# A graph-network kernel on one core: two VectorE steps of its quantile stage cut into pieces of one slot

## The chip, the cores and the metric

The kernel runs on one core of one Trainium2 chip. The metric is the device time of one execution in microseconds (us). Engine names in the profile: PE is TensorE, DVE is VectorE, ACT is ScalarE, POOL is GpSimd, SP is SyncE, which here issues plain DMAs.

## What is computed

Sixteen graphs of 1024 nodes with 64 features each go through four layers. Each layer normalises `x`, clips it at zero and adds the layer's result to `x`. The first three layers are products with the dense 1024 x 1024 matrix `adj` and small weights. The fourth is the one that the change touches:

```python
adj_d = _dilate_adj(adj, mask)      # drops some neighbours of nodes that have more than 10
agg = _weighted_nanquantile_agg(x, adj_d > 0)
out = (1.0 + EPS_GIN) * x + agg
h = jax.nn.relu(jnp.einsum('bnc,ch->bnh', out, W1) + b1)
y = jnp.einsum('bnh,ho->bno', h, W2) + b2
return y * mask[..., None].astype(dtp)
```

The aggregate is, for each node and each feature, the sum 0.25 q(0.25) + 0.5 q(0.5) + 0.25 q(0.75) of interpolated quantiles over the node's remaining neighbours. Neighbours that were dropped count as very large values and sort to the end.

## The kernel before, in words

**Stages.** Six generators yield operations one by one: `listing` makes each node's list of neighbours from rows of `adj` (DVE: `max`, `match_replace`); `transposing` turns blocks of `adj` (PE, ACT); two `layering` workers run layers 1 to 3 for even and odd graphs (mostly PE and ACT) and store a table of features and a payload per graph; `gathering` fetches neighbours' rows from that table with indirect DMAs issued from POOL (80 per graph, one for each of 10 slots and 8 node tiles); `quantiling` sorts and weighs what was gathered; `dense`, added for each graph, multiplies and adds the weighed slots on PE, applies the two small matrices and stores the output.

**The order.** A planner, class `Weave`, holds a cost for every operation (DVE: 0.125 us + elements/960 in most cases; a gather 1.33 us) and lays out each engine's order ahead of time: it issues on the engine that can start first, and among operations that can start within 0.1 us it takes the one with the lowest key. So a change of an operation's length can move other operations on any engine. Where it plans a gap on PE it fills 90% of it with matmuls on a spare bank (line 567). A gather is given a wait on the latest PE instruction that other engines depend on and that the plan has ended before the gather's start (called the leash below). All waits for data come on top.

**Buffers.** Two `G` buffers take turns for the gathered slots, four `pay` buffers hold a graph from the load of `x` to its output, so that the load for graph b + 4 follows the output of graph b; two `row` buffers take rows of `adj` for the listing.

**The quantile stage.** `quantiles` works on cells of 128 nodes x T tiles x 64 features per slot. For a whole graph T is 8 and there are 11 slots, so one slot is 512 elements per partition. First comes `hits`, which finds the dropped neighbours; then their slots get 1e30 added ("bad,G" in the profile); a sorting network of `min` and `max` follows between `G` and `net`; `coef` is computed, and the slots that can hold a quantile are multiplied by it ("G,coef"). The last three places of a whole graph are weighed on ACT (`SHARE`), the others on DVE; `c["weighed"]` tells `dense` how far this has come. After the 16 graphs the nodes whose list stays longer than 11 go through the same stage once more, in four groups (`MANY`): T = 1, 2, 4, 2 with 23, 15, 13, 13 slots. Their outputs are scattered by POOL (line 1245).

**Lengths.** `LONGEST` = 1024 elements bounds a DVE instruction of this stage: `few` = 1024/(T x 64) slots, which is two for T = 8. `parts(k)` cuts k slots into pieces of at most `few`, and it is used for the addition and for the network's steps; the weighing uses `few` by itself.

Of the kernel before, what the change touches and what calls it, by code (L numbers as in the profile page):

```python
# [24 lines left out]
NT = N // P  # L25
# [79 lines left out]
SHARE = 3  # L105
# [349 lines left out]
class Fast:  # L455
# [623 lines left out]
    def quantiles(self, c):  # L1079

        V, S = self.V, self.S
        T, n, PS, G = c["T"], c["n"], c["PS"], c["cells"]

        def small(name, *shape):
            size = int(np.prod(shape))
            t = self.small(name, (P, self.sizes[name]))[:, 0:size]
            return t if len(shape) == 1 else t.rearrange("p (a b) -> p a b", b=shape[1])


        hits = small("hits", (n - 1) * T, 2)  # L1090
        yield V.tensor_tensor(hits.rearrange("p (k t) i -> p k t i", t=T), G[:, 1:n, :, C:R],
                              PS[:, None, :, SELF:SELF + 1].to_broadcast([P, n - 1, T, 2]), op=ALU.is_equal)
        flat = small("bad", (n - 1) * T)
        bad = flat.rearrange("p (k t) -> p k t", t=T)
        yield V.tensor_add(flat, hits[:, :, 0], hits[:, :, 1])
        m1 = small("m1", T)
        yield V.tensor_reduce(m1, bad.rearrange("p k t -> p t k"), axis=AX.X, op=ALU.add)
        yield V.tensor_sub(m1, PS[:, :, COUNT], m1)
        yield S.activation(G[:, 0, :, :], PS[:, :, H:H + R], AF.Copy)


        few = max(1, int(LONGEST / (T * C)))

        def parts(k):
            count = -(-k // few)
            return [slice(k * i // count, k * (i + 1) // count) for i in range(count)]

        for part in parts(n - 1):
            some = slice(part.start * T, part.stop * T)
            there = G[:, 1 + part.start:1 + part.stop, :, 0:C].rearrange("p k t c -> p (k t) c")  # L1110
            yield V.scalar_tensor_tensor(there, flat[:, some, None].to_broadcast([P, some.stop - some.start, C]), BIG, there,
                                         op0=ALU.mult, op1=ALU.add)
        net = yield "net"
        bufs = [w[:, 0:k * T * R].rearrange("p (k f) -> p k f", k=k) for w, k in ((c["G"], n), (net, EXTRA // T))]

        cells = [v.rearrange("p k (t c) -> p k t c", c=R) for v in bufs]


        places = max(int(np.ceil(tau * (n - 1))) for tau in TAUS) + 1
        pos = small("pos", T, 4)  # L1120
        yield V.tensor_tensor(pos, self.taus[:, None, :].to_broadcast([P, T, 4]),
                              m1[:, :, None].to_broadcast([P, T, 4]), op=ALU.mult)
        off = small("off", places, T * 4)
        yield V.tensor_tensor(off, getattr(self, f"place{n}", self.place)[:, 0:places, None].to_broadcast([P, places, T * 4]),
                              pos.rearrange("p t i -> p (t i)")[:, None, :].to_broadcast([P, places, T * 4]),
                              op=ALU.subtract)
        yield S.activation(off, off, AF.Abs)
        yield S.activation(off, off, AF.Relu, bias=1.0, scale=-1.0)

        def side(which, at, ap):  # L1130
            st, d1, n1, d2, n2 = ap
            st += at
            v = bufs[which]
            if n2 == 1:
                return v[:, st, :]
            inner = lambda s: v[:, s:s + d2 * (n2 - 1) + 1:d2, :]
            if n1 == 1:
                return inner(st)
            whole = v[:, st:st + d1 * n1, :] if st + d1 * n1 <= n else None
            if whole is None:  # L1140
                return None
            return whole.rearrange("p (a b) c -> p a b c", b=d1)[:, :, 0:d2 * (n2 - 1) + 1:d2, :]

        if n in NETWORKS:
            for op, k, *sides in NETWORKS[n]:
                for part in parts(k):
                    a, b, o = (cells[st // n][:, st % n + part.start * step:st % n + (part.stop - 1) * step + 1:step, :, 0:C]
                               for st, step in sides)
                    yield V.tensor_tensor(o, a, b, op=getattr(ALU, op))
            self.weave.give("net", net)  # L1150
            where = [(0, SORTED[n][0] + k) for k in range(places)]
        else:
            ops, at = network(n, places)
            for op, ap, dist, ba, bb, bo in ops:
                f = getattr(ALU, op)
                o = (bo, 0 if op == "min" else dist)
                aps = [side(ba, 0, ap), side(bb, dist, ap), side(*o, ap)]
                if any(v is None for v in aps):
                    st, d1, n1, d2, n2 = ap
                    for i in range(n1):  # L1160
                        one = (st + i * d1, 0, 1, d2, n2)
                        yield V.tensor_tensor(side(*o, one), side(ba, 0, one), side(bb, dist, one), op=f)
                else:
                    yield V.tensor_tensor(aps[2], aps[0], aps[1], op=f)
            where = [(at[k], k) for k in range(places)]

        coef = small("coef", places * T)
        yield V.tensor_reduce(coef, off.rearrange("p k (t i) -> p (k t) i", i=4), axis=AX.X, op=ALU.add)
        self.weave.add(self.dense(c, bufs, net, where), c["key"] - 1.0)
        k = 0  # L1170
        while k < places:
            e = k
            while e < places and where[e][0] == where[k][0]:
                e += 1
            e = min(e, k + few)
            v = bufs[where[k][0]][:, where[k][1]:where[k][1] + e - k, :].rearrange("p k (t c) -> p (k t) c", c=R)[:, :, 0:C]
            if T == NT and k >= places - SHARE:
                for i in range((e - k) * T):
                    yield S.activation(v[:, i, :], v[:, i, :], AF.Copy, scale=coef[:, k * T + i:k * T + i + 1])
            else:  # L1180
                yield V.tensor_mul(v, v, coef[:, k * T:e * T, None].to_broadcast([P, (e - k) * T, C]))
            k = e
            c["weighed"] = k
# [718 lines left out]
```

## Time and profile before

| what | value |
|---|---|
| median of 3 runs | 2494.44 us |
| lowest and highest | 2476.52, 2508.35 us |
| profiled execution, its own time | 2479.22 us |
| span in that profile | 2477.4 us |
| mean granted TensorE clock | 0.882 |
| gathers of G from the table on POOL | 1402, from 152 us to 2411 us |
| first and last load of x | 6 and 1795 us |
| table of graph 15 stored | 2039 us |
| gathers of graph 15 | 2080 to 2200 us |
| last `hits` and last `coef` on DVE | 2413.7 and 2457.6 us |

The profile comes from one execution. A row of a group gives line, engine, operation, output and inputs by the program's names, shape and count; then busy time in us and the mean duration of one in ns; then idle time just ahead of it on its engine and what ended most of it. All operations that the planner issues show its line 288, so groups are told apart by tile names. A row of waits gives who waited for whom, the total in us, the number of times and the longest. A row of the timeline gives start, length (of several merged instructions together), engine and operation.

### The profile page before, as it was taken

The page shows a single profiled execution, that of the slowest core. Times are in us where ns is not written, and L with a number is a line of the kernel's source. Part 1 is how long each engine was busy: PE and PEld are TensorE (multiplying, and loading weights), DVE is VectorE, ACT ScalarE, POOL GpSimd, SP SyncE. Part 2 cuts the span into 40 slices and gives each one's busy share as a digit, 9 for nine tenths or more (in the row PEclk, how much of TensorE's full clock was granted, in tenths as well). Part 3 has the DMA queues.
Part 4 walks back from the last instruction along what each step waited for, and adds up shares of the span by engine and source line. Part 5 has one row for each costly group of instructions (what it writes and reads, how often), then busy time and mean ns, then how long its engine had stood idle before and what let it go on. Part 6 is the DMA issues. An engine that isn't in the chain of part 4 may idle for free.

```text
span 2477.4 us, 28435 instructions
## 1 busy us (share of the span) xinstructions
PE 2168.9 (88%) x8704; PEld 955.1 (39%) x8704; DVE 1796.3 (73%) x4505; ACT 935.2 (38%) x2714; POOL 1595.6 (64%) x1441
## 2 busy tenths in 40 slices
PE   8999899999898979897988898989898887779857
PEld 3344334343443333434342434342433333334414
DVE  5878687878696878787878877887777484447553
ACT  4444444354444353535353535353534211101000
POOL 1037676767675767676766676776676677777670
PEclk9999898889897989898989898999897887889969
DMA  6345526262626262616252525262522112121110
GB/s 211 111 112 155 115 65 136 57 138 64 121 74 137 56 160 49 149 39 155 56 133 53 139 65 134 60 146 49 140 38 36 23 35 27 23 28 29 23 24 5
DMA packets 265406, 208.68 MB, mean 84 GB/s; under 512 B 78208, under 2 KB 225984, under 8 KB 265248
## 3 DMA queue, kind: packets, MB, share of 16 engines
q1 hardware_dynamic: 218368, 157.32, 23.3%
q0 software_dynamic: 46096, 48.62, 13.0%
q8 instruction: 72, 1.18, 0.2%
q10 hardware_dynamic: 784, 0.86, 0.1%
q14 instruction: 86, 0.70, 0.1%
HBM read 187.51 MB, written 19.17 MB: 83 GB/s over the span
## 4 chain that ended last, share of the span: by engine, by line
PE 61%; DVE 14%; issue 7%; another core or an unknown queue 7%; ACT 7%; DMA 3%; POOL 1%; SPq 0%; ACTq 0%; DVEq 0%; POOLq 0%
PE bank L288 49%; PE bank L567 13%; DVE G L288 5%; DVE net L288 3%; ACT sq L288 2%; DVE cand L288 1%; DMA block<-in_adj 1%; ACT wide L288 1%; DVE hn L288 1%; DMA pay<-in_x 1%; ACT nodes L288 1%; ACT G L288 1%; DVE st L288 1%; DVE pay L288 1%
## 5 line engine op out<-in xcount | busy, mean ns | idle before, releaser
L613 POOL DMA_INDIRECT G<-table,pay x1402 | 1564.9, 1116 | 812.9 <-issue 374.3
L567 PE MATMUL bank<-ones 128*128 128x512 f16 x2705 | 676.4, 399 | 57.4 <-issue 55.7
L288 PE MATMUL bank<-AT,nodes 128*64 128x512 f32 x2048 | 645.9, 650 | 38.8 <-ACT nodes L288 21.2
L567 PEld LDWEIGHTS <-ones 128*128 128x128 f16 x2705 | 267.6, 102 | 412.6 <-issue 162.8
L288 PEld LDWEIGHTS bank<-AT,nodes 128*64 128x64 f32 x2048 | 171.5, 146 | 374.8 <-issue 286.3
L288 ACT ACTIVATE sq<-pay,st 128x64 f32<-128x64 f32 x512 | 177.1, 346 | 130.1 <-DVE st L288 65.5
L288 DVE MAX8 cand<-key 128x8 f16<-128x128 f16 x1024 | 214.4, 279 | 5.7 <-DVE key L288 2.1
L288 ACT ACTIVATE AT<-bank 128x512 f32<-128x512 f32 x256 | 148.3, 591 | 177.5 <-PE bank L288 131.1
L288 ACT ACTIVATE wide<-bank 64x512 f32<-64x512 f32 x128 | 75.6, 591 | 359.8 <-PE bank L288 253.6
L288 PE MATMUL bank<-c,block 128*128 128x128 f32 x976 | 185.7, 313 | 21.1 <-ACT AT L288 9.1
L288 DVE TENSOR_TENSOR G<-G 128x1024 f32<-128x1024 f32 (+7 forms) x215 | 187.2, 903 | 2.6
L288 PEld LDWEIGHTS bank<-c,block 128*128 128x128 f32 x976 | 127.5, 158 | 159.4 <-issue 135.5
L288 DVE SCALAR_TENSOR_TENSOR key<-row,c 128x1024 f16<-128x1024 f32 x124 | 150.2, 1211 | 38.0 <-DMA row<-in_adj 29.3
L288 PE MATMUL bank<-G,c 128*128 128x512 f32 (+3 forms) x382 | 165.0, 571 | 14.0 <-DVE G L288 7.1
L288 ACT ACTIVATE nodes<-pay,off,ri 128x64 f32<-128x64 f32 x384 | 148.8, 430 | 36.1 <-DVE off L288 15.8
L288 DVE TENSOR_TENSOR yo<-bank,pay 128x256 f32<-128x256 f32 (+2 forms) x36 | 14.8, 411 | 181.5 <-PE bank L288 97.6
L288 DVE TENSOR_TENSOR net<-G 128x1024 f32<-128x1024 f32 (+7 forms) x140 | 141.1, 1033 | 1.3
L288 ACT ACTIVATE G<-G,coef 128x64 f32<-128x64 f32 x384 | 93.8, 336 | 96.8 <-DVE coef L288 96.7
L288 DVE TENSOR_TENSOR G<-net 128x512 f32<-128x512 f32 (+12 forms) x123 | 110.2, 939 | 1.2
L288 DVE MAX8 L<-cand 128x8 f16<-128x64 f16 x384 | 87.4, 228 | 29.2 <-remote 9.7
L288 PE MATMUL bank<-wide,wg 64*64 64x512 f32 (+1 forms) x192 | 105.1, 628 | 3.6 <-ACT wide L288 3.4
L288 DVE TENSOR_TENSOR G<-G,net 128x1024 f32<-128x1024 f32 (+5 forms) x113 | 104.4, 960 | 1.4
(176 smaller groups left out, 2238.4 us busy)
## 6 DMA issues: line engine op xcount, KB each, us to landing
row<-in_adj SPq DMA_DIRECT2D x124, 512.0 KB
block<-in_adj SPq DMA_DIRECT2D x122, 512.0 KB
G<-table,pay POOLq DMA_INDIRECT x1402
rows<-pay SPq DMA_DIRECT2D x16, 632.0 KB
G<-in_adj SPq DMA_DIRECT2D x10, 512.0 KB
table<-pay SPq DMA_DIRECT2D x16, 264.0 KB
pay<-in_x SPq DMA_DIRECT2D x16, 256.0 KB
out<-yo SPq DMA_DIRECT2D x16, 256.0 KB
```

What stands on the lines that cost most here:

```text
L288: return Op(self, lambda: f(*args, **kwargs), writes, reads, cost, later)
L567: weave.spare = (self.T, lambda: nc.tensor.matmul(busy, ones[:, 0:P], ones[:, 0:512], start=True, stop=True), [busy], [ones], 0.22)
L613: return self.nc.gpsimd.indirect_dma_start(out=out, out_offset=None, in_=table, in_offset=bass.IndirectOffsetOnAxis(ap=at, axis=0))
```

## The change

A second bound `alone` is half of `few`. The addition for dropped neighbours is cut by `alone`, and so is DVE's part of the weighing; the sorting network keeps `few`, and so does ACT's part of the weighing, which is done tile by tile anyway. For a whole graph the addition's pieces go from two slots (1024 elements) to one (512), and DVE's six weighed places from three instructions to six. For the four groups of long lists `alone` is 8, 4, 2 and 4 slots, where `few` was 16, 8, 4 and 8.

```diff
         few = max(1, int(LONGEST / (T * C)))
-
-        def parts(k):
+        alone = max(1, few // 2)
+
+        def parts(k, few):
             count = -(-k // few)
             return [slice(k * i // count, k * (i + 1) // count) for i in range(count)]
 
-        for part in parts(n - 1):
+        for part in parts(n - 1, alone):
             some = slice(part.start * T, part.stop * T)
...
             for op, k, *sides in NETWORKS[n]:
-                for part in parts(k):
+                for part in parts(k, few):
...
-            e = min(e, k + few)
+            e = min(e, k + (few if T == NT and k >= places - SHARE else alone))
```

## The prediction

> **What bounds the kernel now.** I read the page's groups first, to see who is loaded and who could set the pace. PE is busy 88% of the span, but 676 us of that is the planner's filler (line 567, 2705 matmuls on a spare bank). POOL has one thing to do:
>
> ```profile
> PE 2168.9 (88%) x8704; PEld 955.1 (39%) x8704; DVE 1796.3 (73%) x4505; ACT 935.2 (38%) x2714; POOL 1595.6 (64%) x1441
> ...
> L613 POOL DMA_INDIRECT G<-table,pay x1402 | 1564.9, 1116 | 812.9 <-issue 374.3
> L567 PE MATMUL bank<-ones 128*128 128x512 f16 x2705 | 676.4, 399 | 57.4 <-issue 55.7
> ```
>
> 1402 gathers one after the other, 1.116 us each, and an idle gap before each. The table of waits splits these gaps:
>
> ```profile
> POOL G L613 <- issue: 374.3, 1149, 5.2
> POOL G L613 <- PE bank L288: 161.7, 132, 10.3
> POOL G L613 <- DMA table<-pay: 135.9, 1, 135.9
> POOL out L1245 <- DVE G L288: 40.7, 1, 40.7
> ...
> DVE hits L288 <- DMA G<-table,pay: 75.3, 7, 32.0
> ```
>
> The columns are total us, times, longest. About 0.3 us of issue stands ahead of nearly every gather and 135.9 us is the start; what is left, 812.9 - 374.3 - 135.9 = 303 us, are waits of the gathers on the leash, which ties them to the PE instruction that the plan has before them. So POOL isn't free-running: 16 times 80 gathers take about 127 us a graph, of which 80 x (1.116 + 0.30) = 113 us is its own work and some 14 us the leash. DVE waits for gathered rows (`hits`) only 7 times, 75.3 us in all, 63.9 of it after 2200 us. Up to there DVE comes to `hits` after the rows have landed. The stretches say the same:
>
> ```profile
> 800.00:1200.00 400.00, 353.96 (x1411) 151.00 (x1412) 315.57 (x791) 181.57 (x519) 280.57 (x250) 0.89 0.42 98
> 1850.00:2203.00 353.00, 286.00 (x1057) 119.58 (x1058) 196.91 (x312) 72.83 (x219) 246.46 (x221) 0.83 0.18 29
> ```
>
> (PE, PEld, DVE, ACT, POOL busy with counts, clock, DMA, GB/s.) In the body PE is at 88% with the filler in its order, DVE at 79%, and POOL at 281 us busy plus 250 x 0.30 = 75 us issue, 89%. PE in plan order, with POOL leashed to it, sets the body. In the tail POOL carries 220 gathers in 353 us, and the 40.7 us wait above holds POOL until DVE's list sort is through: there POOL and DVE alternate.
>
> How DVE lengthens a gather is seen in the timeline, first with DVE's addition for dropped neighbours beside it, then with DVE idle:
>
> ```profile
> 2203.66 5.76 DVE L288 SCALAR_TENSOR_TENSOR G<-bad,G 128x1024 f32<-128x1024 f32 x5
> ```
>
> ```profile
> 2203.92 1.78 POOL L613 DMA_INDIRECT G<-table,pay  x1 [2.45 <-issue]
> 2206.00 1.97 POOL L613 DMA_INDIRECT G<-table,pay  x1 [0.30 <-issue]
> 2208.27 1.97 POOL L613 DMA_INDIRECT G<-table,pay  x1 [0.30 <-issue]
> ...
> 2210.54 0.94 POOL L613 DMA_INDIRECT G<-table,pay  x1 [0.30 <-issue]
> ```
>
> A gather takes 0.94 us alone and up to 1.97 under a 1.22 us addition: it waits for that instruction's end. This is what shorter pieces act on.
>
> [...]
>
> **The change part by part.** Prices come from the groups kept apart by shape:
>
> ```profile
> L288 DVE SCALAR_TENSOR_TENSOR G<-bad,G 128x1024 f32<-128x1024 f32 x83 | 97.0, 1221 | 0.3
> L288 DVE TENSOR_TENSOR G<-G 128x512 f32<-128x512 f32 x92 | 63.2, 687 | 0.8
> L288 DVE TENSOR_TENSOR G<-G,coef 128x1024 f32<-128x1024 f32 x53 | 62.1, 1221 | 0.6
> ```
>
> *Addition, per graph.* 5 x 1221 = 6.11 us becomes 10 x 687 = 6.87, +0.77 us. The half-length addition is not in the trace; its nearest row is the 128x512 `tensor_tensor`, and at 1024 the two operations cost the same. Lower bound: neighbouring instructions overlap (five took 5.76 us, not 6.11, so 0.09 at each seam), and with the same overlap a split costs 153 - 85 = 68 ns, +0.34. I take the upper value.
>
> *Weighing, per graph.* 9 places: the last 3 stay on ACT, 6 on DVE go from 3 to 6 instructions, 3 x 153 ns = +0.46 us. Its cover is ACT: at 2250 us ACT's 24 scalings ran 5.84 us while DVE's three took 3.50 from the same start. PE's product over the places ends with ACT's, so +0.46 is hidden there; without that cover it costs 0.46. What is late next behind it on DVE is whatever the plan put there (a list's `max`, or `hits`).
>
> *The four long-list tiles.* Additions go from 9 to 16 instructions, weighings from 11 to 16: 12 more, near 0.15 each, +1.8 us, nearly all in the tail.
>
> DVE gets 16 x 8 + 12 = 140 more instructions, 128 x 0.153 + 1.8 = +21.4 us busy (lower bound about 10). The order of the built program shows the same 140.
>
> *The gathers.* An addition block of 5.76 us stretched three gathers by 5.72 - 3 x 0.94 = 2.9 us in the case shown; at 1189.64 us, with gaps, five gathers took 5.32 us, 0.6 over. With pieces half as long the wait for the end of one is half: a gain of 0.3 to 1.45 us per graph, I take 0.8; the weighing in proportion (3.5/5.8), 0.5. That is 1.3 us a graph, 21 us over 16 graphs if POOL kept all of it. It doesn't: in the body it arrives earlier at the leash and waits there. In the same timelines, gathers beside the additions already wait 1.28 and 1.34 us for PE. I count body gain 0, bounds -17 and +10 (the latter if the addition's +0.77 delays the PE instructions to which the gathers are leashed, 13 graphs).
>
> *What moves.* The planner lays everything out anew. POOL's order is the same, ACT's and SP's counts too; PE has 2713 fillers instead of 2705, 8 x 0.25 us (676.4/2705) = +2 us. On DVE and SP the last listings slip: the row loads of graph 15 (512 KB each) all come after the store of table 13, where two stood ahead of it, and three of them instead of one stand between the load of x for graph 15 and the store of table 14. On SP that store then waits for DVE's `key` to free row buffers; behind it are the row records and the outputs. Gathers for graph 14 started 1955 us, its table's store was issued at about 1883: some 70 us of cover. I price the slip at 0; with the cover gone it costs the excess.
>
> *Tail.* Graphs 14 and 15 gather under the additions of 13 and 14: 2 x 1.3 = -2.6 us. From `hits` of graph 15 (2202.6) to the first long list's end (2297) DVE is continuous and POOL waits 40.7 us for it: +0.77 + 0.46 + 0.3 = +1.5. Last list: +0.3.
>
> Sum against the profiled execution, 2479.22 us (span 2477.4 and 1.8 around it): +2 filler, 0 body, -2.6 and +1.8 tail, together +1.2, that is 2480. That execution stands 15.2 us below the median of the runs shown, 2494.44; on the median, with nothing claimed in such a difference, 2495.
>
> **The rivals.** *POOL sets the body.* For it: 89% with its issue time, gathers back to back with no wait for the tables after the first. Against it: 303 us of leash waits, and `hits` that isn't waiting. Then the 21 us come, less tail losses: 2494 - 19 = 2475.
> *DVE sets the pace, the slower end.* Place: the chain `hits` to `coef` to PE's list product in every graph, and the load of x four graphs later that waits for the payload tile it frees (x at 1163.23 right after the output at 1162.79). For it: DVE at 79% in the body and shared with the listing. Price: the whole +21 us, 2516. It decides once the leash waits after an addition grow by more than the gathers gained, 1.3 us a graph.
> *The new order costs or gains more than the pieces.* A late listing keeps table 14 or 15 back by over 70 us, or the plan lets PE idle longer in the body: per graph 4 us either way gives 60 us, 2435 to 2555. Filler counts (2713 against 2705) speak against it, as the planned gaps are almost the same.
> *It does nothing:* possible in cost, not in code; the 140 instructions are there.
>
> **How the numbers follow.** Forecast 0.40 (2480 to 2508), POOL 0.14 (2460 to 2485), DVE 0.22 (2505 to 2530), new order 0.24 (two thirds of it slower, nearly all of it beyond 2%, since filler hides little of a wait that the plan doesn't know). About 2% is what a measurement of this kernel can tell from no change: the three runs before span 1.3%. Beyond 2% (under 2445 or over 2544) lies the new-order case: faster 0.08, slower 0.16, within 0.76. The range takes in all of the first three cases and the near ends of the fourth, 2455 to 2540.
>
> **What would show it.** Right: additions x160 and more near 690 ns; gathers' mean below 1.116, near 1.10; their leash waits above 303 us by about as much; body stretches of 400 us again holding about 250 gathers; hits of graph 15 within some us of 2203. POOL rival: over 255 gathers in such a stretch with leash waits unchanged. DVE rival: fewer than 247, and longer waits of POOL on PE. Wrong altogether: `table` stores late enough that gathers wait for them, or PE idle longer with waits on DVE.

## The result, and the profile after

| what | before | after |
|---|---|---|
| median of 20 runs each, us | 2489.37 | 2501.85 |
| lowest to highest, us | 2476.52 to 2510.07 | 2488.39 to 2522.16 |
| profiled execution: span, mean clock | 2477.4, 0.882 | 2511.6, 0.881 |

The ratio of after to before is 1.0071, with a 95% interval of 1.0051 to 1.0091: slower by 0.7%, some 17.7 us, and within the 2% that the prediction counted as no change. The two medians by themselves differ by 12.5 us, or 0.5%. Note that the profiled executions took 2479.22 and 2513.48 us, 10 us below and 12 us above their medians, so of the 34.2 us between the two spans only about half is the change.

The page of the kernel after, engine loads and the groups of the gathers and of the filler:

```profile
PE 2171.9 (86%) x8712; PEld 950.8 (38%) x8712; DVE 1807.5 (72%) x4645; ACT 937.2 (37%) x2714; POOL 1561.4 (62%) x1441
...
L613 POOL DMA_INDIRECT G<-table,pay x1402 | 1531.1, 1092 | 872.4 <-issue 386.5
L567 PE MATMUL bank<-ones 128*128 128x512 f16 x2713 | 681.1, 399 | 71.1 <-issue 70.0
```

DVE has its 140 more instructions and 11.2 us more busy time. A gather has fallen from 1116 to 1092 ns, 33.8 us less in all. But POOL's idle time ahead of the gathers rose by 59.5 us: its gain didn't reach the end. The table of waits (total us, times, longest) says where it went, and that DVE still rarely waits for gathered rows (`hits`, 8 times):

```profile
POOL G L613 <- issue: 386.5, 1116, 6.5
POOL G L613 <- PE bank L288: 210.4, 144, 19.5
...
POOL G L613 <- DMA table<-pay: 135.7, 1, 135.7
...
DVE hits L288 <- DMA G<-table,pay: 67.6, 8, 31.9
...
POOL out L1246 <- DVE G L288: 49.2, 1, 49.2
```

Worked out as in the prediction, the leash holds POOL for 872.4 - 386.5 - 135.7 = 350 us, 47 more than the 303 of before. This counts every wait except issue and the start as the leash. The trace itself puts 210.4 us down to PE, where it was 161.7, and the rest to ACT and others. The new shapes, in the groups kept apart by shape:

```profile
L288 DVE SCALAR_TENSOR_TENSOR G<-bad,G 128x512 f32<-128x512 f32 x172 | 108.0, 692 | 0.3
...
L288 DVE TENSOR_TENSOR G<-G,coef 128x512 f32<-128x512 f32 x107 | 66.9, 691 | 0.6
```

The stretches (columns as in the prediction) show the body at much the same pace, 246 gathers in 400 us where there were 250:

```profile
800.00:1200.00 400.00, 354.17 (x1402) 151.50 (x1401) 308.04 (x797) 179.81 (x516) 270.05 (x246) 0.89 0.42 95
```

**Where the profiled tail lost time.** I cut it at the `hits` of graph 15 and of the first two groups of long lists, all from the timelines of DVE:

| stretch, us | before | after | change |
|---|---|---|---|
| start to `hits` of graph 15 | 2202.6 | 2219.1 | +16.5 |
| to `hits` of the first group | 50.9 | 51.7 | +0.8 |
| to `hits` of the second group | 43.6 | 57.6 | +14.0 |
| to the end | 180.3 | 183.2 | +2.9 |

The third row is the one that stands out. PE's timeline around it, first before, then after (start, length, engine, line, operation, count, idle time ahead of it in brackets). Line 567 is the filler; the 18 matmuls of line 288 are the product over graph 15's weighed slots:

```profile
2170.97 18.91 PE L567 MATMUL bank<-ones 128*128 128x512 f16 x86
...
2205.56 55.61 PE L567 MATMUL bank<-ones 128*128 128x512 f16 x248 [1.52 <-issue]
2261.01 7.89 PE L288 MATMUL bank<-G,c 128*128 128x512 f32 x18
```

```profile
2187.59 18.35 PE L567 MATMUL bank<-ones 128*128 128x512 f16 x82
...
2220.13 0.58 PE L567 MATMUL bank<-ones 128*128 128x512 f16 x1 [2.22 <-issue]
...
2255.75 41.04 PE L567 MATMUL bank<-ones 128*128 128x512 f16 x189 [0.33 <-issue]
2296.63 7.89 PE L288 MATMUL bank<-G,c 128*128 128x512 f32 x18
```

Some 340 fillers are planned into the gap ahead of that product. In both kernels they stall after 80 to 90 of them: single matmuls with mostly 0.3 to 2.9 us of idle "issue" ahead of each, for which the trace shows no releaser. Before, this ends at 2205.56, 3.0 us after the `hits` of graph 15; after, it goes on, with one break, to 2255.75, 36.7 us after them. The fillers take 90.0 us before (2171.0 to 2261.0) and 109.0 us after (2187.6 to 2296.6). Meanwhile the data are ready: ACT ends its share of the weighing at 2255.9 before and at 2272.9 after. The product thus starts 5.1 us after its inputs, and 23.7 us after them in the changed kernel. Behind the product follow the small matrices and, on DVE, the multiplication that finishes the output (`yo`). The plan puts it in the midst of the first long list's sort; here it is in DVE's timeline, before and after:

```profile
2278.45 0.42 DVE L288 TENSOR_TENSOR yo<-bank,pay 128x256 f32<-128x256 f32 x1 [12.23 <-issue]
```

```profile
2310.06 0.43 DVE L288 TENSOR_TENSOR yo<-bank,pay 128x256 f32<-128x256 f32 x1 [26.99 <-issue]
```

DVE stands idle for 27 us instead of 12, with the sort behind it. The 14.8 us between these two waits are the +14.0 of the table's third row. POOL is held as well, since its next gather is on the leash of PE (POOL's timeline, after):

```profile
2297.93 0.94 POOL L613 DMA_INDIRECT G<-table,pay  x1 [19.46 <-PE bank L288]
```

**What may end the stall.** It begins in both kernels while DVE waits for graph 15's rows and POOL gathers at its full pace, 0.94 us and 0.30 of issue each. Here are 5 us out of DVE's additions that follow, before and after (PE, PEld, DVE, ACT, POOL busy with counts, clock, DMA, GB/s):

```profile
2206.00:2211.00 5.00, 4.72 (x17) 1.76 (x16) 4.97 (x8) 0.89 (x2) 4.39 (x3) 0.71 0.08 16
```

```profile
2222.60:2227.60 5.00, 2.00 (x4) 0.31 (x3) 4.96 (x10) 0.51 (x2) 3.78 (x5) 0.50 0.15 28
```

Under the long additions three gathers fall into the 5 us, two of them stretched to 1.97 us, and PE is running again. Beside the short ones five do, unstretched, and PE stays stalled with 4 matmuls in 5 us. So the very gain of the gathers may keep PE's fillers waiting. These are two windows of two traces, and a second place in the tail, shown below, speaks against the pace of the gathers as the whole reason.

**The granted clock doesn't start it.** The first long run of fillers ends at 2189.9 us in before. In the 5 us around that moment the clock is still full, and it falls in the 5 us after it. In after there is also a stretch in which PE has gaps at full clock (first two lines before, third after):

```profile
2186.00:2191.00 5.00, 3.88 (x18) 1.66 (x17) 0.00 (x0) 0.00 (x0) 3.78 (x5) 1.00 0.25 27
2191.00:2196.00 5.00, 0.75 (x2) 0.19 (x2) 0.00 (x0) 0.00 (x0) 3.78 (x5) 0.92 0.27 25
2247.60:2252.60 5.00, 3.45 (x13) 1.08 (x12) 4.97 (x7) 0.00 (x0) 3.84 (x4) 1.00 0.10 20
```

### The profile page after: what moved, and what is told of

It reads as the page before. It is cut to its first block, busy times and chain, and to the rows that moved or that the text cites. A ratio compares the mean times of both kernels' runs of the same rounds, so it can differ in the third digit from the quotient of the medians.

```text
span 2511.6 us, 28635 instructions
## 1 busy us (share of the span) xinstructions
PE 2171.9 (86%) x8712; PEld 950.8 (38%) x8712; DVE 1807.5 (72%) x4645; ACT 937.2 (37%) x2714; POOL 1561.4 (62%) x1441
## 4 chain that ended last, share of the span: by engine, by line
PE 57%; DVE 16%; issue 8%; ACT 7%; another core or an unknown queue 6%; POOL 3%; DMA 2%; SPq 0%; ACTq 0%; DVEq 0%; POOLq 0%
PE bank L288 44%; PE bank L567 12%; DVE G L288 6%; DVE net L288 3%; ACT sq L288 3%; POOL G L613 3%; DVE cand L288 2%; ACT G L288 1%; ACT wide L288 1%; DVE hn L288 1%; DVE key L288 1%; DVE L L288 1%; DVE pay L288 1%; DVE st L288 1%
## 5 line engine op out<-in xcount | busy, mean ns | idle before, releaser
L613 POOL DMA_INDIRECT G<-table,pay x1402 | 1531.1, 1092 | 872.4 <-issue 386.5
L288 DVE SCALAR_TENSOR_TENSOR G<-bad,G 128x512 f32<-128x512 f32 (+1 forms) x176 | 109.9, 689 | 0.3
```

The source lines that it names most:

```text
L288: return Op(self, lambda: f(*args, **kwargs), writes, reads, cost, later)
L613: return self.nc.gpsimd.indirect_dma_start(out=out, out_offset=None, in_=table, in_offset=bass.IndirectOffsetOnAxis(ap=at, axis=0))
```

## The experiments

The theory: the instructions cost next to nothing, the gathers' gain returns to the leash, and what is measured comes from PE's fillers ahead of graph 15's product. The rivals: DVE pays for its 140 instructions (up to 21 us); or the new order costs it, whatever the pieces do. The kernels of one session share a chip and the runs of the kernel before. Before took 2484.93 us (59 runs) in the first session, 2297.21 (53 runs) in the second and 2464.80 (61 runs) in the third, on three different chips. On which chip the first comparison ran is not on record. All ratios are to before in the same session; differences in us are between medians.

### First session: parts of the change, and its order

**Addition alone.** The edit is to the changed kernel.

```diff
-            e = min(e, k + (few if T == NT and k >= places - SHARE else alone))
+            e = min(e, k + few)
```

> Only the addition is cut to pieces of one slot, planned anew; the weighing stays as before. If the added DVE time is what costs (theory DVE): 5 more instructions per graph of the 8, so five eighths of the measured 0.7%, ratio 1.003 to 1.006. If the new order is what costs (theory order): the ratio has no tie to this share; anything from 0.99 to 1.015. If POOL keeps the gain of shorter gathers: below 0.998.

Measured: 2494.77 us, 1.0058 (1.0035 to 1.0080). That fits the theory of DVE and the theory of the order alike, so it doesn't decide between them. The gathers' row:

```profile
L613 POOL DMA_INDIRECT G<-table,pay x1402 | 1530.2, 1091 | 858.7 <-issue 372.8
```

**Weighing alone.** This edit, too, is to the changed kernel.

```diff
-        for part in parts(n - 1, alone):
+        for part in parts(n - 1, few):
```

> Only DVE's weighing is cut to pieces of one slot, planned anew. Theory DVE: three eighths of 0.7%, ratio 1.001 to 1.004, less if ACT's 24 scalings hide it. Theory order: 0.99 to 1.015; this plan has 2814 fillers on PE where before has 2705, which would by itself be +1.1% (109 x 0.25 us = 27 us).

Measured: 2631.97 us (6 runs), 1.0577 (1.0507 to 1.0646), far from every expectation.

```profile
L613 POOL DMA_INDIRECT G<-table,pay x1402 | 1562.9, 1115 | 938.5 <-issue 394.4
```

```profile
POOL G L613 <- PE bank L288: 312.8, 123, 12.0
```

Two things follow. The shorter gathers come from the addition's pieces alone: 1091 ns with them, 1115 with the weighing's, against 1116 before. And the part of the change with the fewer instructions (53 more on DVE) is by far the slowest: POOL waits 312.8 us for PE instead of 161.7, PE has 2814 fillers instead of 2705 and 103.5 us of idle "issue" ahead of them. By elimination that is the work of an order which the planner found for slightly other costs: 53 instructions of 0.15 us can't make 147 us, the 109 fillers make 27 us by the expectation's price, and the next kernel has the weighing's pieces too.

**The same order.** The planner sees the long operation and its cost; the short pieces are issued in its place, so that the order of all else, the fillers and the leashes stay those of before. The weighing is treated likewise.

```diff
-            yield V.scalar_tensor_tensor(there, ...)
+            yield joined(add(part.start, part.stop),
+                         [add(a, min(a + alone, part.stop)) for a in range(part.start, part.stop, alone)])
```

> Both steps are cut as in the changed kernel, but the planner still sees the long instruction, and two short ones are put in its place: every engine has the order of the kernel before. Theory DVE: the instructions cost what they cost, ratio 1.005 to 1.010. Theory order: nothing but the lengths differs, so the cost is gone, 0.997 to 1.002, and below 0.997 if POOL keeps its shorter gathers.

Measured: 2497.35 us, 1.0048 (1.0027 to 1.0069); a gather took 1090 ns. So most of the +0.7% was there in the first session with no change of order: there it is the pieces. And the long stall came with them: it ends 37.3 us after the `hits` of graph 15, the product starts 22.9 us after ACT has ended (2272.0 to 2295.0), and DVE's longest wait of `yo` put down to "issue" is 25.6 us.

**Another order.** The planner's cost of a gather goes from 1.33 to 1.34 us in the kernel before. The work stays the same, but the new plan has 2755 fillers for 2705.

```diff
-GATHER = 1.33
+GATHER = 1.34
```

> The kernel before with the same instructions, but the planner counts 1.34 us for a gather in place of 1.33, which lays out another order (2755 fillers for 2705). Theory order: an order alone moves the time by half a per cent or more, either way. Theory DVE: within 0.3%, but for the fillers, 50 x 0.25 us = 12 us, +0.5%.

Measured: 2500.42 us, 1.0064 (1.0039 to 1.0088). An order drawn anew, with its 50 fillers more (12 us by the expectation's price), costs as much as the whole change. How much of that is the fillers and how much the order isn't separated. A difference of 0.6% between two programs of this planner is therefore no measure of the instructions in them.

### Second session: the tail's fillers, and the number of instructions

**Fewer fillers in the tail**, in before and in after. In gaps before operations of graph 15 and of the long lists, 75% of the gap is filled instead of 90%: 138 and 141 fewer matmuls, no other instruction is added or taken away.

```diff
-                for _ in range(int(FILL * gap / self.spare[4]) if gap > 0.5 else 0):
+                fill = FILL if chain["key"] < GRAPHS - 1 else 0.75
+                for _ in range(int(fill * gap / self.spare[4]) if gap > 0.5 else 0):
```

> The kernel before, with PE's filler before the work of graph 15's output and of the four long-list groups cut from 90% to 75% of the planned gap (138 fillers fewer, 2567); no other instruction or order differs. Theory tail (the added time is lost where PE's filler in the tail runs late and stands ahead of graph 15's product): a little faster, ratio 0.996 to 0.999, since in its profile that product came 5 us after the last scaling. Theory DVE: 0.999 to 1.001.

> The changed kernel with the same lighter filler in the tail (2572). Theory tail: its product for graph 15 came 24 us after the last scaling, so 15 to 20 us come back and it stands at 0.999 to 1.002 of the kernel before, level with the other light one. Theory DVE (the added instructions on the pacing path through all graphs): it stays 0.5 to 0.7% above the kernel before with a light tail, so about 1.004 to 1.007.

Measured: before with it 2301.02 us, 1.0010 (0.9990 to 1.0031); after with it 2283.23 us, 0.9919 (0.9896 to 0.9942). Both expectations missed: that for before lay just below the measurement, and those for after (0.999 to 1.002, or 1.004 to 1.007) lay above it. Before itself took 2297.21 us here, 7.6% less than in the first session, and its own trace, taken for this, shows no stall at all, so that the theory of the tail had nothing to act on:

> The kernel before once more, for a second profile of it: if the wait of graph 15's product behind filler belongs to the kernel, it comes again 3 to 8 us after the last scaling; if it differs by ten us or more, that wait varies from execution to execution and can't be read from one profile.

One run, 2300.17 us. Its rows of gathers and fillers, its waits and the same stretch of its body:

```profile
L613 POOL DMA_INDIRECT G<-table,pay x1402 | 1572.2, 1121 | 648.3 <-issue 334.4
L567 PE MATMUL bank<-ones 128*128 128x512 f16 x2705 | 645.4, 390 | 0.4 <-DVE wg L535 0.4
```

```profile
POOL G L613 <- PE bank L288: 109.7, 144, 12.4
```

```profile
800.00:1200.00 400.00, 371.13 (x1575) 164.16 (x1572) 348.77 (x860) 195.18 (x573) 306.30 (x270) 0.92 0.53 109
```

```profile
2017.93 73.55 PE L567 MATMUL bank<-ones 128*128 128x512 f16 x340
```

The last line is PE's timeline at the place in question: the 340 fillers in one run of 73.55 us, where the same program took 90.0 in the first profile. PE idles 0.4 us ahead of all its fillers where it idled 57.4; 270 gathers fit into the 400 us, not 250; POOL waits 109.7 us for PE, not 161.7. Of the stretch POOL is busy or issuing 306.3 + 270 x 0.24 = 371 us (334.4 / 1402 = 0.24), 93%. So on this chip PE runs without stalls, and POOL is closer to setting the pace. Here the change gains 0.8% once the tail's filler is the same: after is 17.8 us below before (2283.23 and 2301.02), and the gathers' busy time is 40.2 us less (1536.2 and 1576.4). How much of it is the pieces and how much the order isn't separated, and in which stretch it came can't be read, as the profiled execution of the faster kernel was its slowest (2297.13).

**Idle instructions.** Before, with its own order and its long pieces, and behind each piece that the change would split one memset of a single column for each extra instruction, 142 in all, as many as the pieces in the old order add (long pieces split where they stand give two more than the change has). This adds idle work only.

```diff
+                for _ in range(more):
+                    new = self.nc.vector.memset(idle, 0.0)
```

> The order and the long instructions of the kernel before, but after each one that the change would split stands one more DVE instruction that sets a scratch element of one column (140 in all, some 0.07 to 0.15 us each): added DVE time without shorter pieces, so without shorter gathers. Theory DVE: as the short pieces in the same order, 1.004 to 1.010, and more than those if the shorter gathers had given something back. Theory tail, where the gathers' new pace matters and not DVE's: 0.998 to 1.002.

Measured: 2300.68 us, 1.0022 (1.0007 to 1.0038). In the third session the same kernel:

> Long pieces with 140 idle DVE instructions of one column behind them. Quick kind: 1.001 to 1.004 as before. Slow kind, theory DVE (added DVE instructions cost there): 1.003 to 1.008, like the short pieces; theory gathers (there the loss comes from the shorter pieces themselves): 0.998 to 1.002.

2469.33 us, 1.0016 (0.9993 to 1.0040). A memset took 59 ns (groups of the third session's run, kept apart by shape):

```profile
L1114 DVE MEMSET idle<- 128x1 f32 x142 | 8.4, 59 | 0.0
```

They take the place in the order that the extra pieces have, and cost about 0.2%, 3.5 to 4.5 us; a gather is no shorter than before (1120 and 1124 ns). They overlap their neighbours (in the third session's timeline one stands at 2080.95 us under an addition that goes from 2080.93 to 2082.15), so that of their 8.4 us only 0.3 show in DVE's busy time there (1796.6, for 1796.3 in the first profile of before). So this prices the number of instructions. It doesn't price the 11.2 us that the pieces add to DVE's busy time; that stays within what the pieces cost in the old order, 12.4 us in the first session and 4.1 us in the third, stall included.

### Third session: once more on a chip with stalls

> The changed kernel beside the next three on one chip. The chip matters: on the one of the last call the kernel before took 2297 us, PE had no idle time of kind issue before its filler, and gathers hardly waited on the leash; on that of the call before it took 2485 us. If the chip is of the quick kind (before near 2300): theory POOL expects 0.988 to 0.996, since POOL sets the pace there and its gathers get shorter. If it is of the slow kind (before near 2485): 1.005 to 1.009 as in the first comparison.

> Short pieces in the order of the kernel before. Quick kind of chip, theory POOL: 0.988 to 0.996, and level with the changed kernel if the order is no part of it. Slow kind: 1.003 to 1.007 as before.

> The changed kernel with filler at 75% in the tail. Quick kind: as the changed kernel, since its filler isn't late there. Slow kind, theory tail: 15 to 20 us below the changed kernel; theory DVE: level with it.

| kernel | median, us | ratio | interval |
|---|---|---|---|
| after | 2471.97 | 1.0023 | 0.9999 to 1.0048 |
| pieces in the order of before | 2468.92 | 1.0012 | 0.9988 to 1.0036 |
| after, fewer fillers in the tail | 2444.13 | 0.9893 | 0.9857 to 0.9929 |

The change costs a third of what it cost first, with intervals that don't meet, and the pieces in the old order a quarter, with intervals that just do. Both intervals of the third session take in 1, so neither cost can be told from nothing there: the same change was measured at 0.7% once and at 0.2% here. The effect of the fillers is clear: 141 matmuls less in the tail make after 27.8 us faster, and faster than before by 1.1% with the whole interval below 1. But before keeps its full filler in this comparison. PE's timeline of that kernel, where line 568 is the filler:

```profile
2149.52 19.16 PE L568 MATMUL bank<-ones 128*128 128x512 f16 x85
...
2215.33 23.91 PE L568 MATMUL bank<-ones 128*128 128x512 f16 x110 [0.34 <-issue]
2239.08 7.89 PE L288 MATMUL bank<-G,c 128*128 128x512 f32 x18
```

The stall is still there, after 85 fillers, and ends at 2215.33. But fewer fillers are left behind it, and the product starts at 2239.08, 4.1 us after ACT's end. DVE then waits 7.0 us for "yo", where it waited 21.8 us in after on the same chip:

```profile
2252.18 0.42 DVE L288 TENSOR_TENSOR yo<-bank,pay 128x256 f32<-128x256 f32 x1 [7.04 <-issue]
```

From `hits` of graph 15 to the end this trace has 255.5 us; after has 294.0 on that chip and had 292.5 in the first pair, before 274.8. The kernel with idle instructions, which has the long pieces, has 264.6 on that chip.

### The stall in all traces that have one

For graph 15, worked out from the timelines of DVE, PE and ACT: how long after the `hits` of graph 15 the fillers run freely again (the start of the next run of over 100), and how long after ACT's last scaling the product starts.

| kernel, session | additions | stall ends, us after `hits` | product, us after ACT |
|---|---|---|---|
| before, before the sessions | long | 3.0 | 5.1 |
| another order, 1 | long | 5.5 | 9.6 |
| weighing alone, 1 | long | 9.5 | 17.1 |
| idle instructions, 3 | long | 4.0 | 7.7 |
| after, before the sessions | short | 36.7 | 23.7 |
| addition alone, 1 | short | 32.5 | 18.5 |
| pieces in the old order, 1 | short | 37.3 | 22.9 |
| pieces in the old order, 3 | short | 15.2 | 15.7 |
| after, 3 | short | 35.0 | 18.5 |
| after, fewer fillers, 3 | short | 34.1 | 4.1 |

The two kinds don't overlap in the third column: with long additions the stall is over within 10 us of their start, with short ones it lasts 15 to 37 us. At this place it goes with the additions, not with the order (pieces in the old order) nor with the number of instructions (idle instructions) nor with the weighing. The last column follows, but for two rows: in the weighing alone the stall begins 11.2 us into the run of fillers instead of 18 to 19, and in the last row there are fewer fillers to make up.

**A second place.** Ahead of the product of the third group of long lists stands another long run of fillers, 261 of them in before, and it stalls in all ten traces too. Here is before, first PE, then one of POOL's gathers, then DVE:

```profile
2345.26 19.16 PE L567 MATMUL bank<-ones 128*128 128x512 f16 x88
...
2376.41 0.59 PE L567 MATMUL bank<-ones 128*128 128x512 f16 x1 [3.61 <-issue]
2379.21 0.59 PE L567 MATMUL bank<-ones 128*128 128x512 f16 x1 [2.21 <-issue]
...
2407.49 32.82 PE L567 MATMUL bank<-ones 128*128 128x512 f16 x145 [0.82 <-issue]
2440.15 4.48 PE L288 MATMUL bank<-G,c 128*128 128x256 f32 x20
```

```profile
2376.30 1.97 POOL L613 DMA_INDIRECT G<-table,pay  x1 [0.30 <-issue]
```

```profile
2450.17 0.42 DVE L288 TENSOR_TENSOR yo<-bank,pay 128x256 f32<-128x256 f32 x1 [23.68 <-PE bank L288]
```

The `hits` of this group are at 2373.08 us, and before's long additions follow them. Yet the stall goes on for 34.4 us. In after, with short additions, it goes on for 37.8 us after the `hits` at 2401.40. In the ten traces it lasts 34 to 38 us with long additions and 34 to 39 us with short ones, so at this place the pieces make next to no difference. The gather shown is stretched to 1.97 us, and PE stays stalled beside it. From 2105 to 2110 us, in turn, before's gathers run at nearly full pace (0.94 to 1.03 us) while PE goes through 204 fillers without a stall. So the pace of the gathers alone doesn't decide.

In before DVE stands idle for 23.7 us here. On the chip without stalls the 261 fillers ran through in 56.5 us, and PE waited 17.6 us for DVE instead. The fewer fillers act at both places: in the third session DVE's wait for `yo` falls from 21.8 to 7.0 us at graph 15, and from 32.3 to 11.7 us at the third group. Since before has the second wait as well, fewer fillers would probably make it faster too, and the 27.8 us don't measure what the change had lost.

## Why the prediction came out right, and where it was wrong

The forecast was 2495 us with a range of 2455 to 2540; 2501.85 lies inside, and within 2% of before as was said with 0.76. That it came as near as 7 us is in part luck: the forecast starts from the median of three runs, 5 us above that of twenty, and its sum of +1.2 us holds none of the 12 to 18 us that were measured. Step by step:

- *Durations.* The additions take 692 ns and the weighings 691, for 687 from the nearest row; right. DVE's busy time grew by 11.2 us, near the lower bound of about 10 and not the 21.4 that I took: the pieces overlap at their seams, as ten additions of 692 ns took 6.28 us from 2220.15 us on in after, 0.07 less at each seam. The six weighings of graph 15 end after 3.74 us against 3.50 for three, +0.24 where I had +0.46.
- *Gathers.* Their mean was to be near 1.10 and is 1.092. The gain is 33.8 us for 21, and it was divided wrongly between addition (0.8 us a graph) and weighing (0.5): the experiments with one part alone give (1116 - 1091) x 1402 = 35 us to the addition, 2.2 us a graph, and 1 ns a gather to the weighing. That a gather waits for the end of the addition beside it is seen in before: its five additions from 2203.66 us on start 1.13 to 1.14 us apart and take 1.22 each, and the three stretched gathers end at 2205.69, 2207.97 and 2210.24 us, each 0.82 us after the end of the addition in whose course it began.
- *The leash takes the gain back.* Right as a step: leash waits rose by 47 us in the first pair, by more than the gathers gained. The size isn't settled: reckoned the same way, they are 306 us in after's second profile and 337 with the pieces in the old order, for 283 with the idle instructions on that chip. The 303 us were also read too simply, since the trace puts only 161.7 of them down to PE. The body term of 0 held: from 400 to 1600 us 750 gathers before, 744 after, and 769 in after's second trace.
- *The rival that POOL sets the body.* Not in the first pair: no stretch of after shows over 255 gathers. In the third session one does (264), but the kernel with idle instructions has 256 there. On the second chip, where POOL is at 93%, after with a lighter tail gains 17.8 us against before with one, near the 19 us that I gave this rival.
- *The rival that DVE sets the pace.* The size of 17.7 us is near its 21, and its sign, under 247 gathers and longer waits of POOL on PE, appears in one stretch (246; 210.4 us). But after's second trace has 253 gathers in that stretch, and pieces in the old order, with all of DVE's extra work, cost 12.4 and 4.1 us. In the first pair 14.0 us are found at one place of the tail, where DVE was idle.
- *The rival of the new order.* Its mechanism is real and can exceed its price of 60 us, as the weighing alone shows by elimination (+147 us). The change's own order differs from the old order with the same pieces by 0.2% and 0.1%, with intervals that meet: this draw was nearly harmless.
- *Listings that slip* cost nothing, as taken: the table of graph 15 was stored at 2050 us (2039 before), and no gather after the first waits for a table.
- *The step that failed: the tail.* I had -2.6 for shorter gathers under the additions and +1.8 for DVE. The tail from the `hits` of graph 15 grew by 17.7 us in the first pair (that this is the figure of the ratio, too, is chance). The part priced right is in it, +0.8 to the first group's `hits`. Of the rest, 14.0 us are a wait that none of my cases had: PE's 340 fillers, which I priced by number (eight more at 0.25 us), stall, and with short additions they stall longer. I had seen that the fillers idle 57.4 us and passed over it as idle time of filler; but PE issues in the planned order, and the product that DVE and POOL wait for stands behind them. Two lines were misread on the way. DVE isn't continuous from 2202.6 to 2297 us: its 12.2 us wait for `yo` before 2278.45 lies in it. And POOL's wait of 40.7 us isn't in that stretch but from 2411 to 2452 us, at the third group, where DVE itself waits 23.7 us for PE behind stalled fillers.

**What stays open.** Shown is that with the short additions the fillers ahead of graph 15's product stall longer, in every trace that has the stall, and that 141 fewer fillers in the tail take 27.8 us off after. Not shown is that the longer stall is the whole of the +0.7%: before with fewer fillers was not run on a chip with stalls, and the fewer fillers also shorten a stall that before has. The +16.5 us ahead of the tail in the first pair are no more than the scatter of single profiles (in the third session the `hits` of graph 15 stand at 2162.5 us in after, at 2192.2 with the pieces in the old order). Only argued is the link from short additions to the stall, by way of POOL's pace: no run changed that pace alone, and the second place speaks against it. What PE waits for in the stall, and why one chip has none, no trace shows.

## What to carry to other kernels

Work put into a planned gap is priced by what stands behind it in the queue of its engine, and the gap is left slack enough for a chip on which that work runs slower: on a chip with stalls a sixth less filler in the tail gave the changed kernel more than the change had cost it, while on the chip without stalls it did nothing measurable for before (1.0010). Before a small difference is put down to an instruction, run the new instructions in the old order and the old instructions in a new order; with this planner the second alone moved the time by 0.6%. A gain on an engine that is leashed to another can turn into waiting: here the gathers took 33.8 us less in the first pair, and the waits on the leash rose by 47 us. And when a stall is found at one place, look for it at the other places of the same kind, in the kernel before as well: here the second one costs the kernel before 23.7 us.

## What the runs showed of the hardware

- The same program took 2485, 2297 and 2465 us (medians of over 50 runs) on three chips. On the quick one PE idles 0.4 us ahead of its fillers in all, on the others between 40.4 us (idle instructions) and 105.6 us (weighing alone).
- The stall of the tail ahead of graph 15's product begins 18 to 19 us into the run of fillers, after 79 to 87 back-to-back matmuls (51 after 11.2 us in the weighing alone). That at the third group begins in before after 88 matmuls and 19.2 us. A filler takes about 0.22 us before it and mostly 0.38 to 0.59 us within, and PE's granted clock falls to 0.50 within it (after, 2222.6 to 2227.6 us), but only after it has begun (1.00 and 0.92 in the two stretches of 5 us shown above). Not every long run stalls: in before, 204 fillers ran through from 2085.3 us in 44.5 us, with DVE at work beside them.
- A gather is 25 ns shorter on average with additions of 512 elements instead of 1024 (1091 and 1116 ns); halving the pieces of the weighing changed it by 1 ns (1115).
